# The last image's depthwise convolution on the raw input, with the group norm's factor and shift brought in afterwards

## The chip, the cores and the metric

The kernel runs on one core of a Trainium2 chip, in fp32. The metric is the device time of one execution in microseconds (us), the median of several runs.

## The reference

Sixteen images of 384 channels and 32 x 32 positions go through two layers. `_gn` is a group normalisation over 32 groups of 12 channels each.

```python
def _gn(v, G=32, eps=1e-5):
    g = v.reshape(B_, G, C_ // G, H_, W_)
    m = jnp.mean(g, axis=(2, 3, 4), keepdims=True)
    s = jnp.var(g, axis=(2, 3, 4), keepdims=True)
    return ((g - m) / jnp.sqrt(s + eps)).reshape(v.shape)

x = x + attention(_gn(x))        # 8 heads of 48; qkv and projection weights, a bias on the projection
x = x + dwconv7x7(_gn(x), w_sym) # depthwise, padding 3; w_sym = mean of the kernel's four rotations
```

The convolution is linear. Where a channel's normalised plane is s*x + t, its convolution is s times that of x, plus t times the sum of those weights that lie inside the image at each position. That sum depends only on how near a position is to a border: seven kinds of rows and seven kinds of columns.

## The kernel before

Every image is three channel tiles of 128 partitions by 1024 positions, numbered k = 0, 1, 2; after the attention they are `x1s[b, k]`. The loop runs over 16 images, and in each over 64 steps of attention: scores on TensorE (L518), exponentials on ScalarE (L526), values on TensorE (L538). A planner in the kernel (`clock`, `vclock`, `after`, `catch_up`, `tap`) keeps an estimated time for TensorE and VectorE while the program is written out, and puts the convolution of earlier images between the attention's instructions. Each engine then executes its own list strictly in the order written; nothing is reordered on the chip.

The convolution of a tile goes one of two ways.

- On VectorE. ScalarE writes the normalised tile into `padded`, a plane with 35 columns to a row (`fold_x`, L704), and then three products of it into `rows_e` (`fold_first`, L715). `fold_ops` gives 37 operations (38 for the last tile): `side` adds or subtracts a plane shifted left and right (L733), `into` multiplies by a weight and adds (L736), `first` only multiplies (L739), `shifted` adds a finished row sum to the output at a row offset (L746). `tap` puts out one of them at a time.
- On TensorE, for tile 2 of image 14 and tiles 2 and 1 of image 15 (`PE_TILES`). `conv_begin` writes the normalised tile `xn`, by rows of one parity; `conv_store` (L900) stores it to a DRAM plane `xd`, and `conv_load` (L916) reads four overlapping blocks for each half `a` into `sh`. Both are on SP's queue. `conv_on_pe` (L944) convolves with banded matrices, `mats`, which `conv_matrices` (L889) makes on VectorE. `conv_take` (L959) copies the PSUM result to SBUF, and `conv_perm` (L968) puts its rows in order by two matmuls. For image 14 the result is copied by ScalarE (L980), added to `x1s` by an accumulating DMA on POOL (L981) and stored (L823). For tile 1 of image 15, VectorE adds it out of PSUM (`conv_add`, L986) in its own order, and ScalarE's and SP's queues store the halves.

Tile 0 of image 15, called `LAST`, is convolved on VectorE while TensorE does tiles 2 and 1.

In front of that stands the second group norm. For image 15 the residual (L653) is formed on VectorE from the projection in PSUM; VectorE takes the statistics of tiles 1 and 2 by `bn_stats` (L268), ScalarE those of tile 0 (L258 to L264). `groups_on_pe` averages channels over groups by small matmuls with `masks` (L335), first the means and then the deviations `d`. GpSimd (POOL) takes the power -1/2 (L356), and VectorE the shift (L357). Only then do `conv_begin` and `fold_x` normalise. `check_vector`, `check_tensor` and `check_end` test whether the softmax sums were in range; if not, a general version of the kernel, which isn't run with these data, would do everything again.

PSUM is held in two pools: `ps_s`, three tiles of two banks for scores, projections and convolutions, and `ps_o`, two tiles of one bank. The projections of two halves share one tile of `ps_s` (`PPS`): in the second half those of tiles 0 and 1.

Of the kernel before, what the change touches and what calls it, by code (L numbers as in the profile page):

```python
# [10 lines left out]
F32 = mybir.dt.float32  # L11
# [5 lines left out]
P = 128  # L17
# [28 lines left out]
def kernel(  # L46
# [72 lines left out]

    def run(general):  # L120
        tag = "g" if general else "f"
        with ExitStack() as stack:
# [29 lines left out]
            LAST = (B - 1, 0)  # L152

# [93 lines left out]
            class Stats:  # L247
# [5 lines left out]
                def first_channels(self, src):  # L253

                    t = tpool.tile([P, N], F32, tag="t", name=f"sq_{self.name}")
                    s = small.tile([P, 2], F32, tag="s1", name=f"s_{self.name}")
                    self.first = small.tile([P, 2], F32, tag="s2", name=f"mv_{self.name}_0")
                    nc.scalar.activation(t, src, AF.Identity, accum_out=s[:, 0:1])  # L258
                    root = float(N) ** 0.5
                    nc.scalar.activation(s[:, 1:2], s[:, 0:1], AF.Identity, scale=-1.0 / (N * root))  # L260
                    nc.scalar.activation(
                        t, src, AF.Square, bias=s[:, 1:2], scale=1.0 / root, accum_out=self.first[:, 1:2]
                    )
                    nc.scalar.activation(self.first[:, 0:1], s[:, 0:1], AF.Identity, scale=1.0 / N)  # L264
# [56 lines left out]
                def groups_on_pe(self, masks, between=lambda: None, on_pe=lambda: None):  # L321

                    st = small.tile([P, NK, 2], F32, tag="st", name=f"st_{self.name}")
                    if self.first is not None:
                        nc.vector.tensor_copy(st[:, 0, :], self.first)
                    for k in range(self.first is not None, NK):
                        nc.vector.bn_aggr(st[:, k, :], self.bs[:, k, :])
                    ps = ps_o.tile([P, HALF], F32, tag="acc", name=f"ps_st_{self.name}")

                    def average(c0, src):  # L330
                        for mo in range(NK):
                            blocks = [n for n, b in enumerate(MASK_BLOCKS) if b[1] == mo]
                            for n in blocks:
                                ki = MASK_BLOCKS[n][0]
                                nc.tensor.matmul(  # L335
                                    ps[:, c0 + mo : c0 + mo + 1],
                                    lhsT=masks[:, n, :],
                                    rhs=src[:, ki : ki + 1],
                                    start=(n == blocks[0]),
                                    stop=(n == blocks[-1]),  # L340
                                )

                    mean = small.tile([P, NK], F32, tag="mn", name=f"mn_{self.name}")
                    nc.vector.tensor_copy(mean, st[:, :, 0])
                    average(0, mean)
                    on_pe()
                    between()
                    d = small.tile([P, NK], F32, tag="d", name=f"d_{self.name}")
                    nc.vector.tensor_tensor(d, mean, ps[:, 0:NK], ALU.subtract)
                    nc.vector.tensor_tensor(d, d, d, ALU.mult)  # L350
                    nc.vector.tensor_tensor(d, d, st[:, :, 1], ALU.add)
                    average(NK, d)
                    between()
                    nc.vector.tensor_scalar(d, ps[:, NK : 2 * NK], EPS, None, ALU.add)
                    self.sc = small.tile([P, NK, 2], F32, tag="sc", name=f"sc_{self.name}")
                    nc.gpsimd.tensor_tensor(self.sc[:, :, 0], d, mhalf[:, 0:NK], ALU.pow)  # L356
                    nc.vector.scalar_tensor_tensor(  # L357
                        self.sc[:, :, 1], ps[:, 0:NK], -1.0, self.sc[:, :, 0], ALU.mult, ALU.mult
                    )
# [291 lines left out]
            def residual(b, o, h):  # L651
                cols = x1s[b, o][:, h * HALF : (h + 1) * HALF]
                nc.vector.scalar_tensor_tensor(  # L653
                    cols, pps_of(o, h), bp[:, o : o + 1], cols, ALU.add, ALU.add
                )
# [12 lines left out]
            def conv_begin(st, b, k, engine):  # L668
# [9 lines left out]
                else:  # L678
                    dst = xn1s[b, k].rearrange("p (q m w) -> p q m w", q=2, w=W)
                    st.apply(dst, by_rows(x1s[b, k]), k, engine)  # L680
# [43 lines left out]
            def fold_ops(b, k, i):  # L724
# [15 lines left out]

                def shifted(src, dy, op, half=None):
# [3 lines left out]
                    dst = out_t[:, lo:hi]  # L745
                    vec.tensor_tensor(dst, dst, src[:, lo + dy * W : hi + dy * W], op)  # L746
# [12 lines left out]
                outs.append((full, lambda: into(grid(out_t), padded_view(i), e(0, 0))))  # L759
# [43 lines left out]
                while n < len(sums) or m < len(outs):  # L803
# [6 lines left out]
                    else:  # L810
                        ops.append((*sums[n], {0: "x", 3: "rows"}.get(n)))
                        n, out_last = n + 1, False
                return ops

            def half_store(b, k, h):
                c = slice(h * HALF, (h + 1) * HALF)
                (nc.scalar, nc.sync)[h].dma_start(
# [143 lines left out]
            def conv_perm(b, k, a):  # L961
# [14 lines left out]
                if (b, k) == PE_TILES[-1]:  # L976
                    after(13.0, 1.3, lambda: conv_add(b, k, part, (nc.scalar, nc.sync)[a]))
                elif a == 1:
                    t = tpool.tile([P, N], F32, tag="t", name=f"conv_{b}_{k}")
                    nc.scalar.copy(by_rows(t), grids(pss.pop((b, k))))  # L980
                    nc.gpsimd.dma_start(x1s[b, k], t, accum_op=ALU.add)  # L981
                    conv_end(b, k)

# [634 lines left out]
```

## Time and profile before

| | us |
|---|---|
| median of three runs (2856.53 to 2857.79) | 2857.71 |
| the profiled execution | 2858.36 |
| its span, first to last instruction | 2856.6 |
| PE / DVE / ACT / POOL busy | 2833.9 / 2081.7 / 1651.9 / 252.9 |
| last attention matmul ends | 2755.8 |
| last projection matmul ends | 2785.8 |
| last matmul of the convolution ends | 2840.1 |

PE is TensorE's matmuls, DVE is VectorE, ACT is ScalarE, POOL is GpSimd, SP is SyncE, which here only issues DMAs; a q behind the name is the engine's queue issuing a DMA. A line of the timeline gives the start, the duration, the engine, the line of the kernel, the operation with the tile written and those read, how many were merged, and in brackets how long the engine stood idle before it and what ended that. The chain that ended last is followed back from the last instruction to what released each step. Matmuls overlap, so that a busy PE isn't a PE at its peak; what counts is which wait ended last.

### The profile page before, as it was taken

What the parts mean: (1) busy time and instruction counts of PE and PEld (TensorE: products, weight loads), DVE (VectorE), ACT (ScalarE), POOL (GpSimd) and SP (SyncE); (2) the same over time, 40 slices, a digit from 0 to 9 for tenths busy, and PEclk for the clock granted to TensorE, in tenths of its full rate; (3) what the DMA queues carried; (4) which work ended last, traced back from release to release, by engine and by line L of the source; (5) the groups of instructions that cost most, each with busy time, mean ns of one, the idle gap of its engine ahead of it and who ended that gap; (6) DMA issues with size and microseconds to landing.
All of it is one profiled execution on the core that took longest, in us unless ns stands there. A gap on an engine that the chain in (4) does not pass through costs nothing.

```text
span 2856.6 us, 45997 instructions
## 1 busy us (share of the span) xinstructions
PE 2833.9 (99%) x19342; PEld 1118.3 (39%) x19342; DVE 2081.7 (73%) x2255; ACT 1651.9 (58%) x1927; POOL 252.9 (9%) x412
## 2 busy tenths in 40 slices
PE   9999999999999999999999999999999999999997
PEld 5344343433434334343433434334343433434332
DVE  4503968959598695977959598595977959689686
ACT  2637647375574746647476574756647476574731
POOL 3201012210101001010010100001010010100000
PEclk9999999999999999999999999999999999999998
DMA  6612131211212112030211212112130121202223
GB/s 242 189 37 49 32 76 29 54 49 45 64 32 58 43 40 68 27 81 24 50 51 44 64 32 45 54 38 64 34 81 24 44 57 40 68 24 51 59 77 120
DMA packets 75562, 168.40 MB, mean 59 GB/s; under 512 B 31600, under 2 KB 33648, under 8 KB 73808
## 3 DMA queue, kind: packets, MB, share of 16 engines
q0 software_dynamic: 32688, 108.57, 14.6%
q1 hardware_dynamic: 42432, 56.25, 7.2%
q8 instruction: 154, 2.52, 0.4%
q10 hardware_dynamic: 224, 0.52, 0.1%
q14 instruction: 64, 0.52, 0.1%
HBM read 117.09 MB, written 28.68 MB: 51 GB/s over the span
## 4 chain that ended last, share of the span: by engine, by line
PE 98%; issue 1%; DVE 1%; DMA 0%; SPq 0%; POOL 0%; ACT 0%; POOLq 0%
PE ps_s L518 31%; PE acc L538 31%; PE ps_qk L447 17%; PE ps_v L473 9%; PE ps_proj L599 8%; PE ps_conv L944 1%; PE warm L1331 0%; DVE x L746 0%; PE ps_rows L968 0%; PE ps_proj_last L643 0%; DMA sh<-xd 0%; PE ps_st_x L335 0%; DMA xd<-xn 0%; DVE x L986 0%; DVE rows_o L736 0%
## 5 line engine op out<-in xcount | busy, mean ns | idle before, releaser
L526 ACT ACTIVATE e<-ps_s 128x1024 f32<-128x1024 f32 x1024 | 1021.9, 1030 | 448.0 <-PE ps_s L518 446.1
L518 PE MATMUL ps_s<-qk 48*64 48x512 f32 x8192 | 1039.0, 589 | 0.0
L538 PE MATMUL acc<-e,v 64*64 64x512 f32 x8192 | 1038.3, 588 | 0.0
L733 DVE TENSOR_TENSOR side<-padded 128x1024 f32<-128x1024 f32 x270 | 328.7, 1218 | 346.6 <-ACT padded L704 346.6
L736 DVE SCALAR_TENSOR_TENSOR rows_e<-side,even,rows_e 128x1024 f32<-128x1024 f32 x405 | 509.3, 1273 | 85.6 <-ACT rows_e L715 84.1
L518 PEld LDWEIGHTS ps_s<-qk 48*64 48x64 f32 x8192 | 307.9, 132 | 576.3 <-issue 525.9
L538 PEld LDWEIGHTS acc<-e,v 64*64 64x64 f32 x8192 | 309.2, 132 | 572.9 <-issue 572.5
L447 PE MATMUL ps_qk<-x,wqk 128*128 128x512 f32 x1152 | 502.4, 595 | 0.0
L447 PEld LDWEIGHTS ps_qk<-x,wqk 128*128 128x128 f32 x1152 | 218.1, 190 | 277.8 <-issue 272.2
L746 DVE TENSOR_TENSOR x<-x,rows_o 128x992 f32<-128x992 f32 (+3 forms) x271 | 309.7, 1143 | 3.0
L746 DVE TENSOR_TENSOR x<-x,rows_e 128x992 f32<-128x992 f32 (+2 forms) x270 | 310.5, 1150 | 0.0
L454 ACT COPY qk<-ps_qk 128x1024 f32<-128x1024 f32 x96 | 97.2, 1012 | 318.8 <-PE ps_qk L447 318.8
L473 PE MATMUL ps_v<-wv,x 128*128 128x384 f32 x768 | 252.6, 486 | 0.0
L599 PE MATMUL ps_proj<-o,wp 128*128 128x512 f32 x540 | 234.2, 592 | 0.0
L493 ACT COPY v<-ps_v 64x384 f32<-64x384 f32 x256 | 121.6, 475 | 122.4 <-PE ps_v L473 119.9
L473 PEld LDWEIGHTS ps_v<-wv,x 128*128 128x128 f32 x768 | 145.9, 190 | 108.2 <-issue 14.3
L736 DVE SCALAR_TENSOR_TENSOR rows_o<-side,odd,rows_o 128x1024 f32<-128x1024 f32 x135 | 172.7, 1279 | 1.6
L736 DVE SCALAR_TENSOR_TENSOR x<-side,even,x 128x1024 f32<-128x1024 f32 x135 | 172.4, 1277 | 0.0
L823 POOL DMA_DIRECT2D out<-x x46 | 25.9, 564 | 1610.2 <-DVE x L746 1597.9
L599 PEld LDWEIGHTS ps_proj<-o,wp 128*128 128x128 f32 x540 | 102.6, 190 | 126.2 <-issue 118.6
L607 ACT ACTIVATE x<-ps_proj,bp 128x1024 f32<-128x1024 f32 x45 | 50.2, 1115 | 167.4 <-PE ps_proj L599 167.4
L715 ACT ACTIVATE rows_e<-padded,even 128x1024 f32<-128x1024 f32 x135 | 146.8, 1168 | 0.0
(146 smaller groups left out, 1016.4 us busy)
## 6 DMA issues: line engine op xcount, KB each, us to landing
x<-in_x POOLq DMA_DIRECT2D x90, 512.0 KB, 5.5
inv<-inv SPq DMA_DIRECT2D x126, 256.0 KB
out<-x POOLq DMA_DIRECT2D x46, 512.0 KB, 3.0
xs<-in_x POOLq DMA_DIRECT2D x42, 512.0 KB, 6.5
qk<-qk POOLq DMA_DIRECT2D x96, 128.0 KB, 4.1
sh<-xd SPq DMA_DIRECT2D x24, 256.0 KB
o<-o SPq DMA_DIRECT2D x180, 32.0 KB
x<-in_x SPq DMA_DIRECT2D x6, 512.0 KB
```

The costliest lines, as they stand in the source:

```text
L447: nc.tensor.matmul(ps[:, h, :], lhsT=wqk[:, k, s, t, :], rhs=xns[b][:, k, h * HALF : (h + 1) * HALF], start=(k == 0), stop=(k == NK - 1),)
L454: nc.scalar.copy(halves(qks[u][:, s, :]), ps)
L473: nc.tensor.matmul(ps[:, j, 0:C], lhsT=xns[b][:, k, t * P : (t + 1) * P], rhs=wv[:, k, :], start=(k == 0), stop=(k == NK - 1),)
L493: nc.scalar.copy(dst[:, :, 0 : HEADS // 2 * (D + 1)].rearrange("p k (h d) -> p k h d", d=D + 1)[:, :, :, 0:D], src.rearrange("p k (h d) -> ...
L518: nc.tensor.matmul(ps[64 * c : 64 * c + 64, a, :], lhsT=qk[r, 1, 64 * kb : 64 * kb + 64], rhs=qk[r, 0, h * HALF : (h + 1) * HALF], start=True,
L526: nc.scalar.activation(es[n], ps, AF.Exp, scale=SCALE)
L538: nc.tensor.matmul(accs[a][64 * j : 64 * j + 64, :], lhsT=v[rows, kb, c : c + 64], rhs=e[rows, j, :], start=(kb == 0), stop=(kb == 2 * NT ...
L599: nc.tensor.matmul(ps[:, h, :], lhsT=wp[:, t, o * P : (o + 1) * P], rhs=os_[b, t // 2][:, t % 2, h * HALF : (h + 1) * HALF], start=(t == 0 ...
L715: nc.scalar.activation(grid(rows_e[dy - 1]), padded_view(i), AF.Identity, scale=even[:, k, dy, 0:1],)
L733: vec.tensor_tensor(grid(sides[n]), padded_view(i, j), padded_view(i, -j), op)
L736: vec.scalar_tensor_tensor(dst, src, w, dst, ALU.mult, ALU.add)
L746: vec.tensor_tensor(dst, dst, src[:, lo + dy * W : hi + dy * W], op)
```

## The change

The last image is convolved without being normalised, in all three tiles. The copies for TensorE (`conv_begin`) are plain copies of `x1s`, and tile 0's residual is written straight into `padded`. The factor s comes in where results are gathered: as the scale of ScalarE's copy out of PSUM for tiles 2 and 1, and for tile 0 by one operation, `whole`, in the middle of the list; the shifted sums that come after it are multiplied as they are added. The shift t times the border sums is made by ScalarE (nine activations in `factors`) and added by accumulating DMAs into `x1s` of tiles 2 and 1, and into `rest`, a copy of tile 0's input, which `whole` adds. Tile 1's results no longer go through VectorE but the way of image 14. All statistics are taken on ScalarE (`moments`). The border sums themselves are made once by VectorE, together with the matrices `mat_0`, four steps into image 15 instead of sixteen. The second half of the projection takes its tiles in the order 2, 1, 0. Stores that were on ScalarE's queue are on SP's.

```diff
+    def border_sums(t):
...
+        for r in range(EDGES):
+            nc.vector.tensor_reduce(
+                cols[:, :, r, :],
+                wsym[:, :, inside(r), :].rearrange("p k i j -> p k j i"),
+                AX.X,
+                ALU.add,
+            )
+        for r in range(EDGES):
+            at = r if r <= PAD else W - EDGES + r
+            nc.vector.tensor_reduce(border[:, :, :, at], cols[:, :, :, inside(r)], AX.X, ALU.add)
+        nc.vector.tensor_copy(
+            border[:, :, :, PAD + 1 : W - PAD],
+            border[:, :, :, PAD : PAD + 1].to_broadcast([P, NK, EDGES, W - 2 * PAD - 1]),
+        )
...
+                def moments(self, src, k):
...
                     nc.scalar.activation(t, src, AF.Identity, accum_out=s[:, 0:1])
                     root = float(N) ** 0.5
                     nc.scalar.activation(s[:, 1:2], s[:, 0:1], AF.Identity, scale=-1.0 / (N * root))
                     nc.scalar.activation(
+                        t, src, AF.Square, bias=s[:, 1:2], scale=1.0 / root, accum_out=var
+                    )
+                    nc.scalar.activation(mean, s[:, 0:1], AF.Identity, scale=1.0 / N)
...
+                cols, ps = x1s[b, o][:, h * HALF : (h + 1) * HALF], pps_of(o, h)
+                dst = cols
+                if (b, o) == LAST:
+                    dst = padded_view(len(order))[:, h * H // 2 : (h + 1) * H // 2, :]
+                    cols, ps = grid(cols), grid(ps)
+                nc.vector.scalar_tensor_tensor(dst, ps, bp[:, o : o + 1], cols, ALU.add, ALU.add)
...
+                    if b == B - 1:
+                        nc.scalar.copy(dst, by_rows(x1s[b, k]))
+                    else:
+                        st.apply(dst, by_rows(x1s[b, k]), k)
...
+                    dst, src = out_t[:, lo:hi], src[:, lo + dy * W : hi + dy * W]
+                    if scale:
+                        w = scale[0] if op == ALU.add else scale[1]
+                        vec.scalar_tensor_tensor(dst, src, w, dst, ALU.mult, ALU.add)
+                    else:
+                        vec.tensor_tensor(dst, dst, src, op)
+                def whole():
+                    scale.extend((ends["st"].sc[:, k, 0:1], ends["minus"]))
+                    vec.scalar_tensor_tensor(out_t, out_t, scale[0], ends["x"], ALU.mult, ALU.add)
...
+                t = tpool.tile([P, N], F32, tag="t", name=f"conv_{b}_{k}_{a}")
+                src = grids(pss[b, k][part])
+                if b == B - 1:
+                    nc.scalar.activation(
+                        by_rows(t[part]), src, AF.Identity, scale=ends["st"].sc[part, k, 0:1]
+                    )
+                else:
+                    nc.scalar.copy(by_rows(t), src)
+                dst = x1s[b, k][part]
+                nc.gpsimd.dma_start(dst, t[part], accum_op=ALU.add)
+                queue = nc.sync if part.stop < P else nc.gpsimd
                 queue.dma_start(
...
             def fast_end(b):
...
+                for k in PE_K:
+                    conv_begin(st, b, k)
+                    conv_store(b, k)
+                    pe_conv.extend(((b, k, 0, 0, KS), (b, k, 1, 0, 3), (b, k, 1, 3, KS)))
+                fold_first(n, 0)
+                st.moments(padded_view(n), 0)
+                for k in PE_K:
+                    st.moments(x1s[b, k], k)
+                ends["x"] = flat(epool.tile([P, 2, HALF], F32, tag="e", name="rest"))
+                nc.scalar.copy(grid(ends["x"]), padded_view(n))
+                after(4.0, 0.3, check_end)
+                while pe_conv[0][0] < b:
+                    conv_piece(False)
                 conv_piece(False)
+                catch_up(clock)
+                mean, var = st.first
+                st.average(late["masks"], 0, mean)
+                clock += 1.6
+                after(2.5, 0.6, lambda: st.spread_of(mean, var))
+                first = [perms.popleft() for _ in range(2)]
+                for p in first:
                     conv_take(*p)
+                conv_piece(False)
+                for p in first:
+                    conv_perm(*p)
+                catch_up(clock)
+                st.average(late["masks"], NK, st.d)
+                clock += 1.6
+                after(2.2, 0.2, st.scale_of)
+                after(4.5, 0.4, lambda: factors(st))
+                conv_piece(False)
...
+            def factors(st):
+                st.shift_of()
...
+                for k, dst in ((0, rest), *((k, x1s[b, k]) for k in PE_K)):
+                    t = flat(epool.tile([P, 2, HALF], F32, tag="e", name=f"border_{k}"))
+                    for lo, hi in ((0, PAD), (PAD, H - PAD), (H - PAD, H)):
...
+                        nc.scalar.activation(
+                            grid(t)[:, lo:hi, :], src, AF.Identity, scale=st.sc[:, k, 1:2]
+                        )
+                    nc.gpsimd.dma_start(dst, t, accum_op=ALU.add)
...
-                    if once("mat_0", r >= 16):
+                    if once("mat_0", r >= 4):
                         mat = flat2(xpool.tile([P, NK, N], F32, tag="x", name="mat_0"))
                         conv_matrices(0, mat)
                         late["w3"] = mat[:, NG * KS * 2 * CG :][:, 0:C]
+                        late["border"] = border_sums(mat[:, NG * KS * 2 * CG + C :])
+                        vclock += 3.5
```

## The prediction

> **What bounds the kernel now.** I read the page first: its share of busy time and the chain that ended last.
>
> ```profile
> PE 2833.9 (99%) x19342; PEld 1118.3 (39%) x19342; DVE 2081.7 (73%) x2255; ACT 1651.9 (58%) x1927; POOL 252.9 (9%) x412
> PE 98%; issue 1%; DVE 1%; DMA 0%; SPq 0%; POOL 0%; ACT 0%; POOLq 0%
> ```
>
> TensorE holds 98% of the chain, and the edits leave its matmuls alone. Gain or loss can come only from where TensorE is not what ends last: the tail after the last attention step. So next: the chain in order of time, cut to that tail.
>
> ```profile
> 2796.20 0.90 POOL sc_x L356
> 2797.13 0.17 DVE sc_x L357
> 2797.33 0.81 DVE xn L363
> 2798.17 2.84 DMA xd<-xn
> 2803.01 4.65 DMA sh<-xd
> 2807.70 7.54 PE ps_conv L944 x59
> ...
> 2838.11 1.95 PE ps_rows L968 x4
> ...
> 2840.08 1.22 DVE x L986
> ...
> 2849.07 1.19 DVE x L746 x2
> ```
>
> The last projection matmul ends at 2785.75 (timeline of PE: 2783.01 + 2.74). From there the statistics take until 2797.3, then come normalising, the trip through DRAM (store `xd`, loads `sh`), and TensorE's convolution of two channel tiles until 2840.1; VectorE adds its results and finishes tile 0 at 2850.3. The last store is issued at 2850.30, and the span ends 6.3 us later, at 2856.6. The timeline of VectorE shows both idle spells that matter, and an earlier one:
>
> ```profile
> 2667.28 1.23 DVE L733 TENSOR_TENSOR side<-padded 128x1024 f32<-128x1024 f32 x1 [18.66 <-ACT padded L704]
> ...
> 2799.76 1.23 DVE L733 TENSOR_TENSOR side<-padded 128x1024 f32<-128x1024 f32 x1 [1.39 <-ACT padded L704]
> ...
> 2840.08 1.22 DVE L986 TENSOR_TENSOR x<-ps_rows,x 64x1024 f32<-64x1024 f32 x1 [6.39 <-PE ps_rows L968]
> ```
>
> VectorE can't start tile 0 until 2799.76, and later waits 6.4 us, in order, for TensorE. Last, POOL's timeline, since the change puts more there:
>
> ```profile
> 2805.60 0.91 POOL L981 DMA_DIRECT2D x<-conv  x1 [8.51 <-ACT conv L980]
> 2814.42 0.56 POOL L823 DMA_DIRECT2D out<-x  x1 [7.91 <-DMA x<-conv]
> 2830.93 0.88 POOL L981 DMA_DIRECT2D x<-conv  x1 [15.95 <-DVE rows_o L736]
> 2835.90 0.55 POOL L823 DMA_DIRECT2D out<-x  x1 [4.09 <-DMA x<-conv]
> ```
>
> An accumulating DMA of 512 KB is over 5.0 us after its issue when nothing else moves (4.7 us to landing), and 8.8 us among the `sh` loads. In the quiet one, the windows show the DMA engines about fully busy from 2832.0 to 2835.0 (shares 0.68, 1.08, 1.01): some 2.8 us of the 4.7 is transfer, the rest latency.
>
> **What the Trainium skill says.** "DMA: Bandwidth & Descriptors", section "SWDGE vs HWDGE vs iDMA": accumulating during a DMA is only to be had from GpSimd; the trace agrees (L981 is on POOL), so every new accumulation joins POOL's queue. The same page, section "Anatomy of one DMA": waits on semaphores happen at the issuing sequencer; the 7.91 us above is POOL standing still behind one. That section's fit, 2.0 us plus bytes/436e3, would give 3.2 us for 512 KB; plain stores here land in 3.2, the accumulation in 4.7, so I use 4.7. "VectorE: DVE Perf Modes", section on the perf-mode tier table: fp32 `tensor_scalar` from SBUF runs at double rate, two-tensor operations don't; here 0.75 against 1.28 us.
>
> **The change, part by part.**
>
> Mid-kernel. `mat_0` (8 x 0.31 = 2.5 us) and the new border sums (7 reductions, 7 more, one copy of 525 columns; estimate 4 to 5 us from the 0.41 us that a 256-column reduction takes) go on VectorE ahead of L733 at 2667.28. That is inside the 18.66 us of idling: price nothing, and 2.5 us leave a busy stretch. Without that cover it would be 7 us on VectorE, of which 3.7 us of idling before the first residual (2758.5 to 2762.9) would still absorb half.
>
> Start of the tail. Order 2, 1, 0: the residual of tile 2 can run at 2784.05, those of 1 and 0 (one PSUM tile) at 2785.75, 0.7 us each: all done by 2787.2. Four `bn_stats`, the aggregation, the normalising and `fold_x` are gone from the way. So VectorE starts tile 0 at 2787.2 instead of 2799.76: 12.6 us earlier.
>
> ScalarE now holds, in this order: two copies (1.1 each, done 2786.0 and 2787.6), `fold_first` (3.3, to 2790.9), three `moments` (2.75 each, as L258 to L264 took from 2785.72 to 2788.47; to 2799.1), the copy `rest` (1.1), two `rows` (to 2801.3).
>
> SP: the store of tile 2 is issued at 2786.05 instead of 2798.17, 12.1 us earlier; all 16 loads move with it, and their traffic ends near 2803.
>
> TensorE, same instructions, from 2785.75: check 0.1, the rest of image 14's tile (24+16+40 instructions, 8.4) to 2794.2; tile 2's first piece waits about 1.3 us for the loads (2807.70 less 12.1) and ends at 2801.1; averages 1.8, 24 instructions 2.5, four permutations 2.3, averages 1.8, then 3.4 and 6.0: 2818.8. The averages aren't late: the moments are there at 2799.1, and VectorE reaches the `d` operations at 2803.4.
>
> The factor. POOL issues image 14's `x<-conv` at 2808.9 (permutations 2807.7, ScalarE 1.0), and the store behind it waits till 2813.9; the power is behind both, 2814.5 to 2815.4. VectorE is at `shift_of` about 2814.4, so it stands 1 us. ScalarE then does nine border activations, 1.35 us a tile (96, 832 and 96 columns, from L526's 1.03 for 1024 columns and 0.2 for a tiny one), 2815.6 to 2819.7. That reading one repeated row costs more than L526's plain tile no row shows; at 0.5 us a tile more it adds 1.5 to the end, at less than one tile's time it can't gain over 2.0, the wait below. Queued behind these are the two `rows` copies, done 2820.8, and TensorE stands about 2.0 us for them. Then permutations 2.3, 2.5, 1.95, 3.4, a `rows` copy 0.65, 1.95: TensorE ends at 2833.4, before 2840.06.
>
> VectorE in the tail. Its own work on tile 0 is now 50.5 us (2799.76 to 2850.26) less 6.4 wait and 2.4 for L986: 41.7. Add `whole` 1.2, six two-tensor adds that become scaled ones (0.6), small operations (1.4); take 0.5 for the first product: 44.4. From 2787.2, with 1 us of standing, that is 2832.6. `rest` must have landed for `whole`, due near 2821.8 (the first product reads the padded plane: 0.75 us if it keeps L739's rate, 1.28 if not; I take 0.75): border 0 ready 2817.0, issued 2817.3, landed 2822.0. Just in time; 5 us late would still be hidden.
>
> The new end. Tile 1's second half: ScalarE 1.0 (2834.4), accumulation of 256 KB 0.3 + 3.3 (4.7 less half of 2.8), 2838.0; POOL's store at 2838.2 and the end. I bound the last piece between SP's 6.3 and 7.5 (POOL has a register load and a branch behind its store, which no row shows) and take 7.0: 2845.2. VectorE's stores stand on SP behind the first half's store (2835), so end about 2842.
>
> Sum: span 2856.6 to 2845.2, 11.4 us less. The profiled execution took 2858.36, its median sibling 2857.71, 0.65 below it. 2845.2 + 1.76 - 0.65 = **2846.3 us**.
>
> **Rivals.** 0.2% is 5.7 us, about what a measurement of this kernel can tell from no change: faster means below 2852.0.
>
> A: the two TensorE waits close (loads earlier, border work hidden) and the end costs 6.3: 2 + 1.3 + 0.7 less, 2842.3. For it: neither wait is a dependence of arithmetic. Against: ScalarE's order is fixed.
>
> B: image 14's accumulation meets traffic and costs 8.8, as the first one does now; the power, border sums, `rows` and the whole end come 4.1 later: 2850.4, and with 2 us of queueing among the border DMAs 2852.4. Against: the loads are over by 2803.
>
> C, slower: POOL's queue becomes the bound. One place: `rest`, two `border`, `conv` of tile 2 and the two halves of tile 1, five full accumulations. If each ran only after the one before, at x us, the end would be 2812.6 + 6x + 6.6 (the start of `rest`, 2817.3, less 4.7; image 14's accumulation included): 2856.6 at x = 6.2. At the loaded 8.8 it is 2872, a median of 2873. Against: only 2.8 of the 4.7 us occupies the engines, so they overlap, and no loads compete then.
>
> D: that normalisation still comes first is excluded: in the built order both copies and their stores stand ahead of every statistic.
>
> **How the numbers follow.** Forecast 0.62 (2843 to 2849.5), A 0.14, B 0.18, of which 0.08 lies above 2852, C 0.06. Faster 0.86, same 0.08, slower 0.06. The range runs from a little below A to just inside B's upper end, 2841 to 2851.5.
>
> **What would show it.** VectorE's first `side` of tile 0 near 2787 with no wait on ScalarE; no wait on `ps_rows` on VectorE; the `xd` store near 2786; TensorE's last `ps_rows` near 2833; the chain ending through ScalarE and POOL's accumulation. Wrong if `whole` waits more than 6 us for `rest`, if the last accumulation lands after 2844, or if VectorE's last shift ends the span.

## The result, and the profile after

The changed kernel took 2854.14 us, the kernel before 2857.75 us beside it, medians of twenty runs each: a ratio of 0.9989 with an interval of 0.9982 to 0.9995. By the ratio 3.1 us were gained, where 11.4 were forecast. The time lies above the forecast range of 2841 to 2851.5, and by the prediction's own bound of 0.2% it is no change.

Two profiles of the changed kernel are used, called the first and the second below. To compare kernels I use the tail, the time from the end of the last projection matmul, read as the start of the matmul behind it, to the end of the span. The end of the projection itself moves between 2783.5 and 2792.1 us from profile to profile, whatever the kernel, so absolute times mislead. The tail of before is 70.9 us, its forecast for after 59.5. Measured: 71.5 in the first profile (2785.05 to 2856.6), 65.6 in the second (2788.18 to 2853.8).

From the page of the first profile, busy time and the chain that ended last:

```profile
PE 2831.3 (99%) x19342; PEld 1116.2 (39%) x19342; DVE 2079.9 (73%) x2261; ACT 1664.2 (58%) x1951; POOL 264.1 (9%) x418
PE 97%; issue 1%; DMA 1%; POOL 0%; ACT 0%; SPq 0%; POOLq 0%; DVE 0%
```

TensorE still holds nearly all, but VectorE's 1% of the chain has gone to DMA. VectorE's timeline, again of the first profile, shows why:

```profile
2785.15 0.75 DVE L699 SCALAR_TENSOR_TENSOR x<-ps_proj_last,bp,x 128x512 f32<-128x512 f32 x1 [0.97 <-PE ps_proj_last L685]
...
2786.60 1.23 DVE L780 TENSOR_TENSOR side<-padded 128x1024 f32<-128x1024 f32 x1
...
2826.38 1.28 DVE L804 SCALAR_TENSOR_TENSOR x<-x,sc_x,rest 128x1024 f32<-128x1024 f32 x1 [0.84 <-DMA rest<-border]
```

VectorE goes from the residual straight into tile 0, at 2786.60 with no wait on ScalarE (before: 2799.76). It stands 3.10 us for the averages on TensorE, 2.45 for the power on POOL and 0.84 for `rest`, never for the convolution, and is done at 2836.8, twenty microseconds ahead of the end. The edit does what it says. TensorE in the first profile, then in the second:

```profile
2796.65 7.58 PE L1007 MATMUL ps_conv<-sh,mat 128*32 128x512 f32 x50 [2.17 <-DMA sh<-xd]
...
2824.39 3.81 PE L1031 MATMUL ps_rows<-rows,perm 128*64 128x512 f32 x8 [3.32 <-ACT rows L1022]
...
2836.97 1.93 PE L1031 MATMUL ps_rows<-rows,perm 128*64 128x512 f32 x4 [0.70 <-ACT rows L1022]
```

```profile
2822.98 2.42 PE L1031 MATMUL ps_rows<-rows,perm 128*64 128x512 f32 x8 [2.41 <-ACT rows L1022]
...
2833.94 1.93 PE L1031 MATMUL ps_rows<-rows,perm 128*64 128x512 f32 x4 [0.70 <-ACT rows L1022]
```

In the second it ends at 2835.87, 47.7 us into the tail; the forecast's was 47.65. In the first it ends 53.85 us in. The loads made it stand 2.17 us, the piece behind took 7.58 us (5.89 in later experiments), it stood 3.32 behind the border activations, and the permutations after that took 3.81. The windows of the first profile show why those two pieces were slow: the clock granted to TensorE, the first of the last three columns (the others are DMA share and GB/s), drops in just these stretches.

```profile
2795.00:2800.00 5.00, 3.35 (x24) 1.17 (x28) 4.96 (x5) 4.94 (x12) 0.00 (x0) 0.80 1.02 354
2800.00:2805.00 5.00, 5.00 (x38) 1.90 (x30) 2.88 (x3) 0.08 (x1) 0.00 (x0) 0.86 0.59 196
...
2825.00:2830.00 5.00, 5.00 (x24) 1.18 (x26) 4.16 (x4) 1.59 (x2) 0.31 (x2) 0.66 1.05 197
```

In windows of 1 us it is 0.50 from 2798 to 2801 and again from 2826 to 2828; each spell lasts about 3.4 us and costs about 1.7. In the second profile the clock is 1.00 through the permutations of 2.42 us. POOL's timeline, second profile:

```profile
2828.01 0.87 POOL L1052 DMA_DIRECT2D x<-conv  x1 [4.39 <-DMA x<-border]
2834.03 0.57 POOL L1054 DMA_DIRECT2D out<-x  x1 [5.15 <-DMA x<-conv]
2834.59 0.90 POOL L1052 DMA_DIRECT2D x<-conv  x1
2837.36 0.80 POOL L1052 DMA_DIRECT2D x<-conv  x1 [1.87 <-ACT conv L1046]
2842.78 0.56 POOL L1054 DMA_DIRECT2D out<-x  x1 [4.62 <-DMA x<-conv]
```

Since TensorE's end differs so much between the two profiles, a second measure is cleaner: from TensorE's last matmul to the end of the span the forecast had 59.5 - 47.65 = 11.85 us, and both profiles have some six more, 17.7 (2838.90 to 2856.6) and 17.9 (2835.87 to 2853.8). I call it the stretch behind TensorE.

The last accumulation of 256 KB holds the store behind it 5.4 us from its issue, where I had 3.6 plus 0.2. And from that store to the end of the span, 2853.8, it is 11.0 us, where I had 7.0. What POOL does in them is in its queue's instructions, by the lines of the final register load, the branch and the program's end (start of the first and last instruction behind the durations in ns, shortest / median / longest):

```profile
L1677 POOLq TENSOR_LOAD <-again x1: 1248/1248/1248, 2842.8 to 2842.8; - x1
...
L1678 POOLq EVENT_SEMAPHORE  x5: 17/43/43, 2847.2 to 2847.5; - x5
...
L1678 POOLq COMPARE_BRANCH  x1: 58/58/58, 2844.1 to 2844.1; - x1
L1678 POOLq INC_SWDGE_SEM  x1: 1196/1196/1196, 2847.6 to 2847.6; - x1
...
L1722 POOLq DRAIN  x3: 50/98/4152, 2848.8 to 2853.5; - x3
```

A register load of 1.25, some 3.1 from the branch to the semaphores, 1.2 for `INC_SWDGE_SEM`, 4.15 for the longest DRAIN, then the last semaphores. The other engines' last semaphores, too, stand only behind that DRAIN (2855.9 to 2856.5 in the first profile, where it is over at 2855.8). In the profile of before the same items stood in the trace, and the prediction had not used them: POOL's last store came at 2835.90, and its long DRAIN was over at 2845.4, hidden behind VectorE's tile 0.

```profile
L1614 POOLq DRAIN  x3: 50/98/3662, 2841.7 to 2856.3; - x3
```

### The profile page after: what moved, and what is told of

Its sections match the earlier page's. It is cut to its first block, busy times and chain, and to the rows that moved or that the text cites. A ratio compares the mean times of both kernels' runs of the same rounds, so it can differ in the third digit from the quotient of the medians.

```text
span 2856.6 us, 46038 instructions
## 1 busy us (share of the span) xinstructions
PE 2831.3 (99%) x19342; PEld 1116.2 (39%) x19342; DVE 2079.9 (73%) x2261; ACT 1664.2 (58%) x1951; POOL 264.1 (9%) x418
## 4 chain that ended last, share of the span: by engine, by line
PE 97%; issue 1%; DMA 1%; POOL 0%; ACT 0%; SPq 0%; POOLq 0%; DVE 0%
PE ps_s L560 31%; PE acc L580 31%; PE ps_qk L489 17%; PE ps_v L515 9%; PE ps_proj L641 8%; PE warm L1396 0%; PE ps_proj_last L685 0%; PE ps_conv L1007 0%; DMA sh<-xd 0%; DMA x<-border 0%; DMA x<-conv 0%; PE ps_st_x L363 0%; POOL x L1052 0%; DMA xd<-xn 0%; PE ps_rows L1031 0%
## 5 line engine op out<-in xcount | busy, mean ns | idle before, releaser
L799 DVE TENSOR_TENSOR x<-x,rows_o 128x928 f32<-128x928 f32 (+2 forms) x265 | 304.2, 1148 | 3.0
```

The lines of the kernel that those rows point to most:

```text
L799: vec.tensor_tensor(dst, dst, src, op)
```

## The experiments

The theory after the first profile: POOL's ending, which I priced at 7.0 us, is the largest part of the loss, and the slow last accumulation and TensorE's stands are the rest. (In that profile TensorE's lateness, 6.2 us, was in fact the larger term; the next run shows that it doesn't always come.) The rivals: TensorE alone decides; image 14's accumulation holds the factor up; VectorE's own list ends the tail. A number with "ratio" is to the kernel before, run beside it, with the 95% interval.

**The changed kernel once more** (no edit).

> The changed kernel again, for a second profile: the first profiled execution (2858.4 us) is among the slowest of its twenty, whose median is 2854.1. Theory 1: the runs differ in the tail, where transfers meet. Then the last attention matmul ends at 2755 to 2756 here too, and a span of 2849 to 2855 comes out of the time after it, with POOL's last store still some 10.9 us before the end. Rival: the runs differ in the attention part; then the last attention matmul moves by as much as the span and the tail stays at 101 us.

Ratio 0.9994 (0.9988 to 1.0001), tail 65.6. This is the second profile above. Both theories were half right: the projection ended 3.1 us later than in the first profile, and the tail was 5.9 us shorter. The lateness of TensorE in the first doesn't come in every execution; POOL's ending of 11.0 us is in both (10.9 in the first).

**Tile 1's second half stored by SP.**

```diff
-                queue = nc.sync if part.stop < P else nc.gpsimd
+                queue = nc.sync if (b, k) == PE_TILES[-1] else nc.gpsimd
```

> The changed kernel with one edit: the last store, of tile 1's second half, is on SP's queue instead of POOL's. Theory 1 (POOL's own ending is long: 10.9 us from its last store to the end of the span, against 6.3 from SP's last store in the kernel before): SP's store starts when the accumulation lands and the end comes 6.3 us later, while POOL's ending counts from its last accumulation; 4 to 5 us less than the changed kernel, about 2849.5. Rival (the 10.9 us are the landing of the transfers, whoever issues them): within 1 us of the changed kernel, 2853 to 2855.

Ratio 0.9985 (0.9977 to 0.9993), tail 63.3. TensorE ended late in this profile (50.0 us into the tail), but the stretch behind it is 13.3 us instead of 17.9: 4.6 us, about as much as POOL's ending is above SP's. By the timed ratios it is 2.6 us, with intervals that just overlap. The last lines of SP's timeline and of POOL's, and the DRAIN in POOL's queue:

```profile
2842.22 0.80 SPq L1054 DMA_DIRECT2D out<-x  x1
```

```profile
2836.61 0.80 POOL L1052 DMA_DIRECT2D x<-conv  x1 [2.35 <-ACT conv L1046]
```

```profile
L1722 POOLq DRAIN  x3: 50/98/4070, 2843.5 to 2848.1; - x3
```

The span ends at 2848.4, 6.2 us behind SP's store. POOL's last DMA is now the accumulation, 11.8 us from the end, and POOL's long DRAIN is over at 2847.6, 0.8 us before the end as in the changed kernel. So both queues end together, and no more was left to gain from the store: POOL's ending counts from its last DMA of any kind.

**The kernel before, with its last store on POOL** (tile 0's second half, from SP's queue).

```diff
-    (nc.scalar, nc.sync)[h]
+    (nc.scalar, nc.gpsimd)[h]
```

> The kernel before with one edit: its very last store, the second half of tile 0, is issued by POOL instead of SP. Theory 1: the ending behind POOL's last DMA is 10.9 us instead of 6.3, so 4 to 5 us slower than before, about 2862. Rival (POOL's ending in the changed kernel was long because of traffic): 0 to 1 us slower.

Ratio 1.0008 (1.0001 to 1.0014). From POOL's timeline:

```profile
2852.88 0.55 POOL L817 DMA_DIRECT2D out<-x  x1 [14.20 <-DVE x L746]
```

The span ends at 2862.6, 9.7 us behind this store; SP's took 6.3. That shows the price in the kernel before: 3.4 us more than from SP. The tail is 4.2 us longer, as expected; by the timed ratio the cost is some 2 us. POOL's ending is 1.3 us shorter than in the second profile of the changed kernel. Part of that goes with the number of POOL's DMAs, with which the longest DRAIN grows: 3.66 us in the kernel before, 3.74 here with one more, 3.91 in three kernels below with three more, 4.07 in three kernels with five more, 4.15 in the changed kernel with six more. That is 0.08 us each, 0.4 of the 1.3. The register load took 0.5 more in the second profile (0.1 in the first), and the way from the branch to the semaphores 0.3.

**Tile 2's `rows` copies ahead of the border activations.**

```diff
                 after(4.5, 0.4, lambda: factors(st))
                 conv_piece(False)
+                for p in perms:
+                    conv_take(*p)
+                    taken.add(p)
```

> The changed kernel with one edit: ScalarE copies tile 2's convolution rows out of PSUM ahead of the nine border activations instead of behind them. Theory 1 (TensorE's chain sets the end, and its 3.3 us of standing and the slow permutations after it, 3.8 us instead of 2.3, lie on it): TensorE doesn't wait there, and the end comes 4 to 5 us earlier than in the changed kernel, about 2849.5. Rival (the accumulations queued on POOL set the end, whatever TensorE does): 0 to 1 us less.

Ratio 0.9988 (0.9981 to 0.9994). TensorE no longer stands; it ends 44.9 us into the tail, 2.8 earlier than in the second profile. But the tail stays at 66.0, the stretch behind TensorE grows to 21.1, and POOL's timeline says where it went:

```profile
2829.25 0.87 POOL L1052 DMA_DIRECT2D x<-conv  x1 [4.38 <-DMA x<-border]
2835.45 0.57 POOL L1054 DMA_DIRECT2D out<-x  x1 [5.33 <-DMA x<-conv]
2836.00 1.73 POOL L1052 DMA_DIRECT2D x<-conv  x2
2843.65 0.56 POOL L1054 DMA_DIRECT2D out<-x  x1 [5.92 <-DMA x<-conv]
```

Tile 2's accumulation still waits for the border's landing, its store for that, and tile 1's accumulations stand behind the store on POOL. By ScalarE's timeline its last copy even waits 4.07 us for an accumulation, though its PSUM is ready. So with TensorE early, POOL's queue sets the end, and taking away TensorE's stand alone gains nothing that these runs show.

**Image 14's store on SP**, behind all loads, so that the power isn't behind its accumulation.

```diff
-                queue = nc.sync if part.stop < P else nc.gpsimd
+                queue = nc.sync if part.stop < P or b < B - 1 else nc.gpsimd
...
                 conv_piece(False)
+                loads(2)
```

> The changed kernel with image 14's last store taken off POOL's queue and put on SP's, behind all sixteen loads, so that the power no longer stands behind an accumulation. Tail means here the time from the end of the last projection matmul to the end of the span; it is 71.5 and 65.6 us in the two profiles of the changed kernel, 70.9 before. Theory 1: VectorE's stand of 1.1 to 2.5 us at the shift goes, the border activations come that much earlier, and so does the end: tail 1 to 2.5 us under the changed kernel's in the same job, about 64. Rival (the three border accumulations and tile 2's, one after the other on POOL's queue, set the end from there on): the same direction, but all of POOL's four later accumulations move together with the power and TensorE's chain doesn't matter; if neither, the tail stays at 65.6.

Ratio 0.9979 (0.997 to 0.9989), tail 67.1 in a profile with 1.6 us of standing for the loads. The power no longer waits for the accumulation, but it runs while that is still under way, and takes 2.84 us instead of 0.91:

```profile
2815.48 0.87 POOL L1052 DMA_DIRECT2D x<-conv  x1 [38.95 <-ACT conv L1050]
2818.53 2.84 POOL L381 TENSOR_TENSOR sc_x<-d_x,mhalf 128x3 f32<-128x3 f32 x1 [2.17 <-DVE d_x L380]
```

VectorE's stand for it is 0.79 us (1.09 in the second profile). Here profile and timed runs don't agree on the sign, and I draw only this from it: the wait that was taken away was largely given back. Whether the accumulation lengthens the power is not shown. VectorE worked for 2.08 of the 2.84 us here, and for none of the 0.91 us in the changed kernel, where it stood waiting for the power; no run separates the two.

**Tile 1 added by VectorE out of PSUM**, times the factor, behind tile 0, four operations of 64x512 (L1067), and stored by SP; tile 2 and image 14 as in the change.

```diff
+                for q in range(2):
+                    nc.vector.scalar_tensor_tensor(
+                        dst[:, q], src[:, q], ends["st"].sc[part, k, 0:1], dst[:, q], ALU.mult, ALU.add
+                    )
```

> The changed kernel with tile 1's convolution added by VectorE straight out of PSUM, times the factor (four operations of 64 partitions x 512 behind all of tile 0's), and stored by SP: one part of the change undone. Theory 1: the path behind TensorE shrinks from ScalarE 1.1 + accumulation 5.4 + POOL's ending 11.0 to VectorE 1.5 + SP's ending 6.3; POOL's last DMA is then tile 2's store, some 46 us into the tail, and its ending of 11 sets the end: tail about 57, 8 to 9 us less than the changed kernel, a time near 2846 where before is 2858. Rival (the accumulations ahead and TensorE's chain hold VectorE as well): VectorE's adds wait for tile 1's border accumulation or for TensorE beyond 50 us into the tail, tail 61 or more.

Ratio 0.9962 (0.9951 to 0.9974), tail 57.8. With the two last accumulations gone the tail is 7.8 us shorter than in the second profile, with TensorE ending as late as there (48.0); the stretch behind it is 9.8 us instead of 17.9. That is the strongest evidence for where the forecast's gain went: not TensorE, but what came behind it, and here the timed ratio's interval is clear of the changed kernel's too. POOL's last DMA, tile 2's store at 2834.49, is 11.4 us from the end, SP's last, at 2839.0, 6.9: the two endings are again close.

**The same, with image 14's and tile 2's stores on SP too.**

> As the kernel with VectorE's add, and the stores of image 14's tile and of tile 2 moved from POOL's queue to SP's behind all loads. Theory 1: POOL's last DMA is then tile 2's accumulation, about 39 us into the tail, its ending is over at 51, and the end is TensorE's last permutation (47.7) + 1.5 + 6.3: tail 55 to 56, 10 us less than the changed kernel, some 12 to 15 us faster than before. Rival (POOL's ending doesn't count when something else is late): the same tail as with POOL's stores, within 1 us.

2845.93 us against 2860.25 beside it, ratio 0.9952 (0.9939 to 0.9965), tail 56.6; the interval overlaps the one just shown. This version beats both kernels. VectorE and SP at its end:

```profile
2831.70 2.86 DVE L1067 SCALAR_TENSOR_TENSOR x<-ps_rows,sc_x,x 64x512 f32<-64x512 f32 x4 [0.48 <-PE ps_rows L1031]
```

```profile
2833.12 1.98 SPq L1070 DMA_DIRECT2D out<-x  x2
```

VectorE stands 0.48 us for TensorE's last permutation, and the span ends at 2840.9, 6.3 us behind SP's last store (2834.6). POOL's last DMA was at 2823.80, so its ending is hidden.

**SP's last stores put in another order**, tile 1's second half first.

> The changed kernel with the order of SP's last stores turned round: tile 1's second half first, then its first half, then tile 0's. So nothing but tile 2's store can move data while the last accumulation of 256 KB is under way. The prediction took 3.6 us for it; the profiles of the changed kernel show 5.3 to 5.4. If traffic makes the difference, it is 3.5 to 4.3 us here; if an accumulation of 64 partitions takes as long as one of 128, it is 5.0 or more. The end itself comes 3 us or so later, since the other stores wait.

2852.25 us in one run, tail 64.9. The accumulation of the second half took 5.26 us from its issue to the store (2836.22 to 2841.48). But it wasn't alone: tile 2's store and the first half's accumulation, issued at 2832.77 and 2833.33, still moved, and the share of the DMA engines stood between 0.7 and 1.1 from 2834 to 2840. So this run didn't answer what it was made for, and the next does.

**All stores of the last image held back**, tile 1's second half first among them, image 14's on SP.

```diff
-                queue = nc.sync if part.stop < P else nc.gpsimd
-                queue.dma_start(
+                def store():
+                    queue = nc.sync
+                    queue.dma_start(
...
+                if b == B - 1:
+                    held.insert(0, store)
+                else:
+                    store()
```

> The changed kernel with all stores of the last image on SP and put behind everything, tile 1's second half first, and image 14's store on SP behind the loads. Then no store of tile 2 or of tile 1's first half moves while tile 1's second half is accumulated; before, each profile of the changed kernel had some 0.5 MB of tile 2's store and the first half's accumulation moving next to it. It tells apart what made that accumulation of 256 KB 5.3 to 5.4 us long from its issue, where the prediction had 3.6. Theory 1 (traffic ahead of it): 3.3 to 4.0 us from the start of POOL's issue to SP's issue of the store that waits for it, and DMA share near 1.0 for less than 2 us. Theory 2 (an accumulation takes the same time whatever its size, since its half tile spreads over the engines worse): 4.8 to 5.4 us again, with the share near 1.0 for 2.5 us or more.

One run, 2851.25 us. The accumulation goes alone; POOL's issue and SP's store behind it (the first of three):

```profile
2834.02 0.81 POOL L1054 DMA_DIRECT2D x<-conv  x1 [5.17 <-ACT conv L1048]
```

```profile
2839.23 1.87 SPq L1057 DMA_DIRECT2D out<-x  x3
```

It is 5.2 us again. The time is what theory 2 said. The windows of this kernel around the 256 KB, and of the kernel before around its quiet 512 KB (stretch, its length, busy time of PE, PEld, DVE, ACT and POOL, granted clock, DMA share, GB/s):

```profile
2834.80:2839.30 4.50, 0.00 (x0) 0.00 (x0) 0.00 (x0) 0.00 (x0) 0.03 (x1) 0.83 0.61 69
```

```profile
2831.00:2836.00 5.00, 5.00 (x36) 1.40 (x36) 2.69 (x3) 0.12 (x1) 0.91 (x2) 1.00 0.57 108
```

0.61 of 4.5 us is 2.7 us of busy engines; 0.57 of 5.0 is 2.9. Half a tile's accumulation keeps the engines busy about as long as a whole one's, at about half the rate. By the DMA view the two windows hold 64 and 128 packets of 4 KB, so that one packet held an engine for some 0.64 us in the half tile and 0.35 in the whole (estimates: the accumulation's share of 57.2% and 55.6% over 16 engines, divided by the packets). Theory 2's reason, a worse spread over the engines, is not shown. My halving of the transfer was wrong by itself, with no traffic needed.

**The change without the shift's part**: the nine border activations and their three accumulations are left out, so the output lacks the shift times the border sums.

> The changed kernel without the shift's part: the nine border activations and their three accumulating DMAs are left out, so that the output lacks the shift times the border sums; everything else stays. It prices that part. Tail of the changed kernel in its second profile: 65.6 us, POOL's ending 11.0 us of it. Theory (the border part costs only TensorE's stand behind ScalarE, 2.4 us, and POOL's ending stays as long as before): TensorE ends near 45 us into the tail, POOL's last store follows some 9.6 us later, and the tail is 62.5 to 64, the median 2 to 3 us below the changed kernel's. Rival (three accumulations fewer in the queue let tile 2's and tile 1's accumulations go through at once, and shorten POOL's ending): tail 60 or less, last accumulation issued to landed in under 4.5 us. Second rival (nothing is gained, the end is set by something else, VectorE or SP): tail 65 to 66.

Ratio 0.9972 (0.9966 to 0.9979), tail 62.2. TensorE ends 45.2 into it, 2.5 earlier, and POOL's last store, at 2844.05, is 10.25 from the end (11.0), the longest DRAIN 3.91 instead of 4.15. The first theory was close in the tail, 0.3 too high at its lower end; by the timed ratios the part costs more, 0.17 to 0.22%, 5 to 6 us. Tile 2's accumulation, with no border DMA near, still holds its store 6.4 us (2828.38 to 2834.78), and tile 1's first half stands behind that store, so the queue isn't freed by leaving three DMAs out.

**VectorE's adds, with the `rows` copies ahead of the border**: the version that beats both, and besides the edit of tile 2's `rows` copies.

> The version in which VectorE adds tile 1's results and the last two POOL stores stand on SP, and besides ScalarE copies tile 2's `rows` ahead of the nine border activations. Tail means from the last projection matmul's end to the end of the span; the version without the second edit had 56.6 us, with TensorE ending 47.4 us into it. Theory (TensorE's end now sets the tail, POOL's queue no longer): TensorE stands 2.0 us less and doesn't slow down after the wait, so ends 44.5 to 45.5 us into the tail, VectorE's four adds follow, tail 53.5 to 55, and a median of 2843 to 2844.5, ratio near 0.9944. Rival (VectorE's own list for tile 0, which waits for `rest`, sets the end of the tail as soon as TensorE is early, because the border activations are 1.3 us later): the tail stays between 56 and 57.5, ratio 0.9950 or above.

Ratio 0.9953 (0.9937 to 0.997): no better. The tail is 57.5, as the rival had it. TensorE ends 46.6 into it, with 1.88 us of standing for the loads, and VectorE comes to the adds later than that, without a wait:

```profile
2840.34 2.86 DVE L1067 SCALAR_TENSOR_TENSOR x<-ps_rows,sc_x,x 64x512 f32<-64x512 f32 x4
```

The line has no bracket, so VectorE didn't wait: its own list for tile 0 now ends last, and TensorE's end, 0.7 us earlier than in the version without the edit, buys nothing. The rival's reason, later border activations, isn't what the profile shows. VectorE had the factor (`sc_x`, L384) 30.9 us into the tail instead of 29.4, ahead of any border activation, and was 1.4 to 1.5 us late from there on; TensorE's stand for the loads, 1.88 us against 0.23 without the edit, had come before the averages. Without that stand there were at most the 0.48 us to gain for which VectorE waited in the version without the edit.

**The kernel before, with the mid-kernel part alone** (`mat_0` earlier, and the border sums, which nothing reads here).

```diff
-                    if once("mat_0", r >= 16):
+                    if once("mat_0", r >= 4):
...
+                        late["border"] = border_sums(mat[:, NG * KS * 2 * CG + C :])
+                        vclock += 3.5
```

> The kernel before with the mid-kernel part of the change alone: `mat_0` four steps into image 15 instead of sixteen, and the border sums made there (here nothing reads them). It prices that part, which the prediction put at nothing because VectorE idles 18.66 us ahead of L733 at 2667.28. Theory (hidden): ratio within 0.999 and 1.001, tail from the last projection matmul's end to the end of the span near 71 us as before, and the idle of VectorE ahead of that L733 shorter by about 7 us. Rival (the later work on VectorE is displaced, so that the residual or the tail come later by 2 us or more): ratio 1.0007 or more, and either the projection's end or the tail 2 us later.

Ratio 1.0002 (0.9993 to 1.0011), tail 70.5. VectorE's idle in mid-kernel, ahead of the `side` that stood at 2667.28 in before (L733, here L760), is 12.06 us, 6.6 less than 18.66; about 7 had been expected:

```profile
2670.11 1.23 DVE L760 TENSOR_TENSOR side<-padded 128x1024 f32<-128x1024 f32 x1 [12.06 <-ACT padded L731]
```

## Why the prediction was wrong, point by point

- **The mid-kernel part: nothing.** Right, and shown by itself: ratio 1.0002.
- **The start of the tail.** Right. VectorE starts tile 0 at 2786.6 (2787.2 forecast), and the store of tile 2 is issued at 2785.34 (2786.05). Some twelve microseconds are really gained there.
- **TensorE, 47.65 us to its end.** Right in the second profile (47.7), too low in the first (53.85). The agreement is partly luck: in the second profile the rest of image 14's tile and tile 2's first piece took 15.5 us together, where the sum had 8.4 and 5.6, and the 1.3 us of standing for the loads between them didn't come. (The terms as written also add up to 0.15 more than the 2833.4.) The stand for the `sh` loads, 1.3 in the sum, was between 0 and 2.2 us from profile to profile. The stand behind ScalarE's border work, 2.0 in the sum, was 2.4 and 3.3, and the permutations behind it, 2.3, took 2.4 and 3.8. The first profile's two spells of half the clock, with about 1.7 us lost in each, are in no term of the sum. Rival A had both stands gone; the run with the copies first shows that the end wouldn't have followed.
- **The factor.** The border activations took 4.40 us for nine (4.05), image 14's accumulation 5.2 and 6.1 from issue to store (5.0 forecast; rival B's 8.8 didn't come). B's 4.1 us had set 8.8 to the store behind it against 4.7 to landing; like for like it would have been 3.8. The measured time lies above 2852, where B had its upper part, but not for B's reason.
- **VectorE's tail.** Right in kind: no wait for TensorE's convolution any more, `rest` in time (0.84 us of standing), and never the end.
- **The new end.** This is the step that failed, in two terms. The last accumulation: "256 KB 0.3 + 3.3 (4.7 less half of 2.8)", 3.6; it measured 5.4 and 5.3, and 5.2 when nothing else moved. The last piece: "I bound the last piece between SP's 6.3 and 7.5 [...] and take 7.0"; it measured 11.0 and 10.9. Between TensorE's end and the accumulation's issue lie 1.5 us instead of 1.0. In the second profile these make the whole difference: 1.6 + 4.0 + 0.5 = 6.1, and 59.5 + 6.1 = 65.6. Of the signs that the prediction named, the chain did end through ScalarE and POOL's accumulation; the last accumulation was over at 2845.7 in the first profile, behind the 2844 that was to show it wrong, and at 2842.8 in the second.
- **Rival C**, POOL's queue as the bound, was ruled out too quickly on the ground that accumulations overlap. They do, but a store that waits on POOL holds back the next accumulation (tile 1's first half stood 3.5 us in the second profile, from the end of its copy at 2831.04 to 2834.59), and with the copies first the queue alone set the end. The count of five accumulations also took the two halves of tile 1 for one, while each takes as long as a whole. The queue didn't make the kernel slower.

The bound of 7.5 had been set by a register load and a branch, "which no row shows". The trace of before did show them, and `INC_SWDGE_SEM` and DRAIN after them, in the lines of POOL's queue behind its last store at 2835.90. They added up to 9.5 us there, and cost nothing only because VectorE worked on for longer.

**What stays open.** Profiles and timed runs don't give one number. By profile the tail of the changed kernel is 0.6 us longer or 5.3 shorter than that of before; the gains by the timed ratios lie between, at 3.1 and 1.7 us. The first profiled execution took 4.2 us more than the median of its runs, the second 4.3 us less. So the new end's 6.1 us are shown for a fast execution; that the other 2 to 4 us missing by the timed runs are TensorE's lateness fits the first profile, but is not shown for the median run. The stand for the loads lay between 0 and 2.2 us in eleven profiles of the changed kernel and its variants, none of which moves the `xd` stores, and no run settled what sets it. Nor is it settled when the clock drops: it did behind a stand of 2.17 us in the first profile, and didn't behind one of 2.41 in the second. Putting the second `xd` store behind the first loads wasn't tried.

## What to carry to other kernels

Before a last store or accumulation is moved to another engine's queue, follow that engine in the trace of the kernel as it is, from its last DMA to its last instruction: that stretch may be hidden now and become the end. Don't scale the time of an accumulating DMA by bytes when the trace has none of the smaller shape; take the full one's time. When a wait is removed at one engine, read which queue the results pass through next, in order, before the gain is counted. When a piece of TensorE's work is longer in one profile than in another, read the granted clock in that stretch first.

## What the runs showed of the hardware

- POOL's ending, from its last DMA to the end of the span where POOL's is the one that ends last: 9.7 to 11.4 us behind a store, 11.8 behind an accumulation. SP's: 6.2 to 6.3. The longest DRAIN grew by 0.08 us with each further POOL DMA, from 3.66 to 4.15.
- An accumulation of 256 KB into 64 partitions took as long as one of 512 KB into 128: 5.2 us to the store behind it against 5.0, with the engines busy for 2.7 us against 2.9.
- The power of 128x3 on POOL took 2.84 us instead of 0.91 in the four kernels where it ran while an accumulation was still under way and VectorE worked for 2.08 us of it; behind the landing, with VectorE standing idle, it took 0.91. Which of the two lengthens it is open.
- TensorE's eight permutations took 1.94 us with no idle before them, and 2.41 to 2.42 after 1.7 to 2.4 us of it, at a granted clock of 1.00. After 2.75 to 3.5 us of it they took 3.60 to 3.81, at a granted clock of 0.57 to 0.62 in that stretch.
